# Two graph layers on one core: where the row factors, the group ends and the copies out of the banks are done

## The chip, the cores and the metric

The kernel runs on one core of a Trainium2 chip. The metric is the device time of one execution in microseconds (us). The core has TensorE (PE, matrix products), VectorE (DVE), ScalarE (ACT) and GpSimd (POOL), each working through its own list of instructions in order, and SyncE (SP), whose list here holds only transfers. Transfers are also issued from ScalarE's and GpSimd's lists. All of them run on the core's 16 DMA engines.

## The reference

A graph of 4096 nodes with 512 features goes through two layers. Each takes relu(layernorm(x)) and adds the outcome to x. Layer 0 is an attention with a full score matrix; layer 1 is an attention with 8 heads of 64, whose score is a sum of a row's and a column's number.

```python
def _L0_gnn_ref(x, adj, weight, bias, node_w, edge_w):
    node_att = jax.nn.softmax(x @ node_w, axis=0)
    h = x @ edge_w
    e = h @ h.T
    e = jnp.where(adj > 0, e, NEG_BIG)
    edge_att = jax.nn.softmax(e, axis=1)
    combined_att = node_att * edge_att
    support = x @ weight
    return adj * combined_att @ support + bias

def _L1_gnn_ref(data, connectivity, W, b, src_proj, trg_proj):
    data1 = (data @ W.T + b).reshape(N, H, D)
    src = jnp.einsum('nhd,xhd->nh', data1, src_proj)
    trg = jnp.einsum('nhd,xhd->nh', data1, trg_proj)
    e = src.T[:, :, None] + trg.T[:, None, :]
    e = jnp.where(e >= 0, e, 0.01 * e)
    e = e + connectivity[None, :, :]
    scores = jax.nn.softmax(e, axis=-1)
    out = jnp.einsum('hnm,hmd->hnd', scores, data1.transpose(1, 0, 2))
    return out.transpose(1, 0, 2).reshape(N, H * D)
```

In this model adj is passed as the connectivity of layer 1. All is in 32-bit floats.

## The kernel before

It has four stages, one after the other in time.

**Layer 0, first pass** (until about 745 us): layer norm, the products he_t and sup, the logits of the nodes, then the scores e, of which one half is computed and written to DRAM (e_d), and the masked maxima of the rows (mx_d). The change does not touch it.

**Layer 0, second pass** (about 745 to 1747 us). 8 blocks b of 512 rows (BL), each with 32 steps m of 128 columns. The order of work is written out by hand in `stages` (L332): in loop step s, `load` works for step s+8, `turn` for s+3, `exps` for s+2, `weigh` for s+1 and `gather` for s. `load` fetches scores (et or eb) and the transposed adjacency (a) through SP. `turn` lets TensorE transpose the scores that exist only mirrored. `exps` makes the mask, subtracts the maximum and adds the mask on VectorE (L279, L282, L283) and exponentiates on ScalarE (L285). `weigh` multiplies with the adjacency on VectorE (L291, tile at) and sums the rows on GpSimd (L301, racc). `gather` lets TensorE add at times sup into four PSUM banks po0 to po3 (L324), which are held once (c_p, bufs=1).

At a block's first step `gather` also loads four tiles xt of x through SP and lets GpSimd add the bias to them (L311). At its last step it sums racc with four small products (L318, rs), and VectorE makes sc from rs (L320, L321) and then, straight out of each bank, ot = po * sc + xt (L328); GpSimd's queue writes ot to x1 in DRAM (L330).

**Layer 1, preparation** (to about 1915 us): layer norm of x1, the projected values va, and the factors by which the exponential of leaky relu splits into a maximum of products. Each row's factor z goes to DRAM (z_d).

**Layer 1, main part** (1915 us to the end). A group is 1024 rows (WL) and four of the eight heads; there are 8 groups of 32 steps m. `stages` (L582): `load` for step s+3, `exps` for s+1, `weigh` for s+1, `factors` for s+2, `gather` for s. In each step:

- SP loads a tile e of the adjacency (L452, three buffers);
- ScalarE makes ex (L465, into two PSUM banks held once, so it must wait until VectorE has used the ex before), then e3 and rl of the step after (L474, L477);
- VectorE makes four products pr3, pr0, pr1, pr2, in this order (L489, L486, L489, L489), from z, rl, e3 and ex;
- GpSimd adds pr3 to acc3 (L498), and an accumulating transfer on its queue adds pr0 to acc0 or acc1 (L504);
- TensorE multiplies the products with va into four banks (L516) and sums pr1 and pr2 in dn (L522).

Row factors z are needed as four tiles [128, 1024] per group, the same row in all partitions (`zload`, L461, on GpSimd's queue, 6 buffers): 3 and 0 are asked for with the group's first load, 1 and 2 with its first `factors`.

After a group's last step ScalarE copies the four banks and dn out (os L531, od L532). The rest of the ending is the generator `finish`, of which one piece runs in each step from the fourth of the next group on (L587 to L590): transposes of od and reciprocals rd on VectorE (L543, L544); six sums of the accumulators (L553 to L556) with their copy oa (L558) on ScalarE; again transposes and reciprocals; then four pairs of row tiles, for each a load y of x1 on ScalarE's queue (L567), four transposes (L572), o = pt * rd (L575), two additions of o to y (L577, L578) on VectorE, and the transfer to out on ScalarE's queue (L579). The transposes share one bank, pt. The last group's ending has no next group beside it (L591).

Of the kernel before, what the change touches and what calls it, by code (L numbers as in the profile page):

```python
# [8 lines left out]
FP = mybir.dt.float32  # L9
AF = mybir.ActivationFunctionType  # L10
ALU = mybir.AluOpType
# [4 lines left out]
P = 128  # L16
# [6 lines left out]
def row_bcast(ap, n, offset=0):  # L23

    return bass.AP(tensor=ap.tensor, offset=ap.offset + offset, ap=[[0, P], [1, n]])
# [3 lines left out]
def kernel(  # L29
# [15 lines left out]
    nc = tc.nc  # L45
    N, F = x.shape
    H, D = 8, 64
    HG = 4
    NT = N // P
    KC = F // P  # L50
    BL = 512
    NB = N // BL
    TB = BL // P
# [3 lines left out]
    ident = const.tile([P, P], FP, name="ident")  # L57
# [4 lines left out]
    x1 = dram.tile([N, F], FP, name="x1")  # L62
    z_d = dram.tile([H * NT, P], FP, name="z_d")
# [27 lines left out]
    na = big.tile([P, NT], FP, name="na")  # L91
# [9 lines left out]
    with tc.tile_pool(name="w0", bufs=1) as wp, tc.tile_pool(name="a0", bufs=2) as ap_, tc.tile_pool(  # L101
        name="a0s", bufs=4
    ) as sp, tc.tile_pool(name="a0p", bufs=2, space=PSUM) as pp, tc.tile_pool(
        name="a0l", bufs=1, space=PSUM
# [115 lines left out]
    with tc.tile_pool(name="c_e", bufs=9) as etp, tc.tile_pool(name="c_b", bufs=4) as ebp, tc.tile_pool(  # L220
# [12 lines left out]
        def rows_of(m):  # L233
            return slice(m * P, (m + 1) * P)
# [69 lines left out]
        def gather(b, m):  # L304
            if m == 0:
                blk[b][2] = [p_o.tile([P, F], FP, name=f"po{j}") for j in range(TB)]
                blk[b][3] = []
                for j in range(TB):
                    xt = iop.tile([P, F], FP, name="xt")
                    nc.sync.dma_start(xt, x[rows_of(b * TB + j), :])  # L310
                    nc.gpsimd.tensor_tensor(xt, xt, bias_b, ALU.add)  # L311
                    blk[b][3].append(xt)
            mb, racc, po, xts = blk[b]
            last = m == NT - 1
            if last:
                rs = p_r.tile([P, TB], FP, name="rs")
                for j in range(TB):
                    nc.tensor.matmul(rs[:, j:j + 1], racc[:, j * P:(j + 1) * P], ones, start=True, stop=True)  # L318
                sc = sp.tile([P, TB], FP, name="sc")
                nc.vector.reciprocal(sc, rs)  # L320
                nc.vector.tensor_tensor(sc, sc, na[:, b * TB:(b + 1) * TB], ALU.mult)  # L321
            w = at.pop((b, m))
            for j in range(TB):
                nc.tensor.matmul(po[j], w[:, j * P:(j + 1) * P], sup[:, m, :], start=(m == 0), stop=last)  # L324
            if last:
                for j in range(TB):
                    ot = iop.tile([P, F], FP, name="ot")
                    nc.vector.scalar_tensor_tensor(ot, po[j], sc[:, j:j + 1], xts[j],  # L328
                                                   op0=ALU.mult, op1=ALU.add)
                    nc.gpsimd.dma_start(x1[rows_of(b * TB + j), :], ot)  # L330

        stages = ((load, 8), (turn, 3), (exps, 2), (weigh, 1), (gather, 0))  # L332
        for s in range(-8, len(steps)):
            for f, ahead in stages:
                if 0 <= s + ahead < len(steps):
                    f(*steps[s + ahead])
    l0.close()


# [91 lines left out]
    WL = 1024  # L431
# [3 lines left out]
    with tc.tile_pool(name="e", bufs=3) as ep, tc.tile_pool(name="e3", bufs=2) as e3p, tc.tile_pool(  # L435
# [13 lines left out]
        def load(i, m):  # L449
            b, g = groups[i]  # L450
            e = ep.tile([P, WL], FP, name="e")
            nc.sync.dma_start(e, adj_t[m * P:(m + 1) * P, b * WL:(b + 1) * WL])  # L452
            ra[i, m] = e
            if m == 0:
                zload(i, 3)
                zload(i, 0)

        def zload(i, k):
            b, g = groups[i]
            zs_[i, k] = zp.tile([P, WL], FP, name="z")  # L460
            nc.gpsimd.dma_start(zs_[i, k], row_bcast(z_d, WL, (g * HG + k) * N + b * WL))  # L461

        def exps(i, m):
            x_ = p_x.tile([P, WL], FP, name="ex")
# [41 lines left out]
        def gather(i, m):  # L506
            b, g = groups[i]
            if m == 0:
                pv[i] = ([[p_v.tile([P, BL], FP, name=f"pv{c}{q}") for q in range(HV)] for c in range(2)],
                         p_v.tile([P, BL], FP, name="dn"))  # L510
            v, dn = pv[i]
            flags = dict(start=(m == 0), stop=(m == NT - 1))
            for c, pair in enumerate(((3, 0), (1, 2))):
                for q in range(HV):
                    for r, k in enumerate(pair):
                        nc.tensor.matmul(v[c][q][r * D:(r + 1) * D, :], va[:, m, g * HG + k, :],  # L516
                                         pr[i, m, k][:, q * BL:(q + 1) * BL], **flags)
            for k in (1, 2):
                d = d_m[:, g * HG + k, m:m + 1]
                for q in range(HV):  # L520
                    r = (k - 1) * 2 + q
                    nc.tensor.matmul(dn[r * Q:(r + 1) * Q, :], d.to_broadcast([P, Q]),  # L522
                                     pr[i, m, k][:, q * BL:(q + 1) * BL], **flags)
            for k in range(HG):
                pr.pop((i, m - 1, k), None)
            if m == NT - 1:
                os_ = [[osp.tile([P, BL], FP, name=f"os{c}{q}") for q in range(HV)] for c in range(2)]
                od = osp.tile([P, BL], FP, name="od")
                for c in range(2):
                    for q in range(HV):  # L530
                        nc.scalar.copy(os_[c][q], v[c][q])  # L531
                nc.scalar.copy(od, dn)  # L532
                late[i] = os_, od

        def finish(i):
            b, g = groups[i]
            os_, od = late.pop(i)
            rd = sp.tile([P, WT, HG], FP, name="rd")

            def dens(src, two):  # L540
                pt = p_t.tile([P, WT // HV, P], FP, name="pt")
                for j in range(WT // HV):
                    nc.tensor.transpose(pt[:, j, :], src[:, j * P:(j + 1) * P], ident)  # L543
                nc.vector.reciprocal(rd[:, :, two].rearrange("p (q j) k -> p j k q", q=HV),  # L544
                                     pt.rearrange("p j (k q d) -> p j k q d", k=2, q=HV)[:, :, :, :, 0])

            dens(od, slice(2, 4))
            yield

            ps = p_t.tile([P, BL], FP, name="pt")  # L550
            for q in range(HV):
                s = slice(q * BL, (q + 1) * BL)
                nc.tensor.matmul(ps[q * Q:(q + 1) * Q, :], ones, acc[i, 3][:, s], start=True, stop=True)  # L553
                r = HV + q
                nc.tensor.matmul(ps[r * Q:(r + 1) * Q, :], ones, acc[i, 0][:, s], start=True, stop=False)
                nc.tensor.matmul(ps[r * Q:(r + 1) * Q, :], ones, acc[i, 1][:, s], start=False, stop=True)  # L556
            oa = osp.tile([P, BL], FP, name="oa")
            nc.scalar.copy(oa, ps)  # L558
            yield
            dens(oa, slice(0, 2))  # L560
            yield
            for j in range(0, WT, 2):
                rows = slice(b * WL + j * P, b * WL + (j + 2) * P)
                y = iop.tile([P, 2, HG, D], FP, name="y")

                cols = slice(g * HG * D, (g + 1) * HG * D)
                nc.scalar.dma_start(y, x1[rows, cols].rearrange("(j p) (h d) -> p j h d", p=P, h=HG))  # L567
                pt = p_t.tile([P, 2, HG, D], FP, name="pt")
                for q in range(2):
                    for c in range(2):  # L570
                        s = (j + q) * P % BL
                        nc.tensor.transpose(pt[:, q, 2 * c:2 * c + 2, :].rearrange("p k d -> p (k d)"),  # L572
                                            os_[c][(j + q) * P // BL][:, s:s + P], ident)
                o = sp.tile([P, 2, HG, D], FP, name="o")
                nc.vector.tensor_tensor(o, pt, rd[:, j:j + 2, :].unsqueeze(3).to_broadcast([P, 2, HG, D]),  # L575
                                        ALU.mult)
                nc.vector.tensor_tensor(y[:, :, 0:3, :], y[:, :, 0:3, :], o[:, :, 1:4, :], ALU.add)  # L577
                nc.vector.tensor_tensor(y[:, :, 3, :], y[:, :, 3, :], o[:, :, 0, :], ALU.add)  # L578
                nc.scalar.dma_start(out[rows, cols].rearrange("(j p) (h d) -> p j h d", p=P, h=HG), y)  # L579
                yield  # L580

        stages = ((load, 3), (exps, 1), (weigh, 1), (factors, 2), (gather, 0))  # L582
        for s in range(-3, len(steps)):
            for f, ahead in stages:
                if 0 <= s + ahead < len(steps):
                    f(*steps[s + ahead])
            if s > NT and s % NT == 3:  # L587
                ending = finish(s // NT - 1)
            if s > NT and s % NT >= 3:
                next(ending, None)  # L590
        for _ in finish(len(groups) - 1):  # L591
            pass
# [34 lines left out]
```

## Time and profile before

| | |
|---|---|
| time, median of 3 runs | 3289.96 us (3289.59 to 3289.97) |
| the profiled execution's own time | 3290.54 us |
| its span, first to last instruction | 3288.7 us, granted TensorE clock 0.981 |
| TensorE busy | 3117.9 us (95%) |
| VectorE busy | 2573.5 us (78%) |
| GpSimd busy | 1415.7 us (43%) |
| ScalarE busy | 1195.6 us (36%) |
| product into the banks, L516 | 1025.2 us, 4096 of 610 ns |
| product of the second pass, L324 | 915.2 us, 2048 of 598 ns |
| VectorE products L489 and L486 | 1285 us, 1024 of about 1274 ns |

The span is the time from the first to the last instruction of one profiled execution. A busy share is an average over four stages with different limits, and the busy time of TensorE counts matmuls that are pipelined, so that 95% does not say that TensorE is the limit everywhere. The table of slices shows this: in the second pass DMA is busy for about 0.4 to 0.5 of the time and VectorE for 0.6 to 0.8; in layer 1 both are at 0.8 to 0.9 or more.

```profile
PE   8999999998999999999998869999999999999997
PEld 4554444444444444444444423232323232323332
DVE  3324777776667678788896599898989898999997
ACT  2211111111111111111113256565656666666664
POOL 0001111113434445445454546565656565655554
PEclk9999999998999999999999989999999999999999
DMA  2104666656444444454433179898988898989896
```

Each digit is one fortieth of the span (82 us), in tenths.

### The profile page before, as it was taken

What the parts mean: (1) busy time and instruction counts of PE and PEld (TensorE: products, weight loads), DVE (VectorE), ACT (ScalarE), POOL (GpSimd) and SP (SyncE); (2) the same over time, 40 slices, a digit from 0 to 9 for tenths busy, and PEclk for the clock granted to TensorE, in tenths of its full rate; (3) what the DMA queues carried; (4) which work ended last, traced back from release to release, by engine and by line L of the source; (5) the groups of instructions that cost most, each with busy time, mean ns of one, the idle gap of its engine ahead of it and who ended that gap; (6) DMA issues with size and microseconds to landing.
All of it is one profiled execution on the core that took longest, in us unless ns stands there. A gap on an engine that the chain in (4) does not pass through costs nothing.

```text
span 3288.7 us, 34545 instructions
## 1 busy us (share of the span) xinstructions
PE 3117.9 (95%) x11514; PEld 1291.8 (39%) x11514; DVE 2573.5 (78%) x3593; ACT 1195.6 (36%) x1417; POOL 1415.7 (43%) x1081
## 2 busy tenths in 40 slices
PE   8999999998999999999998869999999999999997
PEld 4554444444444444444444423232323232323332
DVE  3324777776667678788896599898989898999997
ACT  2211111111111111111113256565656666666664
POOL 0001111113434445445454546565656565655554
PEclk9999999998999999999999989999999999999999
DMA  2104666656444444454433179898988898989896
GB/s 74 39 20 158 225 219 229 223 182 211 142 141 155 142 157 159 141 163 157 147 107 103 36 188 223 228 218 225 219 224 217 222 223 224 222 227 219 227 221 161
DMA packets 239250, 577.07 MB, mean 175 GB/s; under 512 B 26048, under 2 KB 51936, under 8 KB 239072
## 3 DMA queue, kind: packets, MB, share of 16 engines
q1 hardware_dynamic: 163680, 357.76, 32.7%
q0 software_dynamic: 55680, 196.13, 26.9%
q10 hardware_dynamic: 19712, 20.98, 2.1%
q8 instruction: 90, 1.47, 0.2%
q14 instruction: 88, 0.72, 0.1%
HBM read 389.02 MB, written 51.53 MB: 134 GB/s over the span
## 4 chain that ended last, share of the span: by engine, by line
PE 62%; DVE 18%; issue 6%; ACT 6%; DMA 4%; POOL 2%; ACTq 0%; DVEq 0%; SPq 0%; POOLq 0%
PE po L324 26%; PE pe L180 14%; DVE pr L489 13%; PE pv L516 8%; ACT e L474 5%; PE ps L136 3%; PE pe L129 3%; PE dn L522 2%; DMA z<-z_d 2%; PE pd L382 2%; PE pt L271 2%; DMA y<-x 1%; POOL pr L387 1%; PE lg L139 1%; DVE d L283 1%
## 5 line engine op out<-in xcount | busy, mean ns | idle before, releaser
L516 PE MATMUL pv<-pr,va 128*64 128x512 f32 x4096 | 1025.2, 610 | 61.5 <-DVE pr L489 40.2
L324 PE MATMUL po<-sup,at 128*128 128x512 f32 x2048 | 915.2, 598 | 45.1 <-DVE at L291 45.1
L498 POOL TENSOR_TENSOR acc<-acc,pr 128x1024 f32<-128x1024 f32 x240 | 570.3, 2376 | 434.2 <-DVE pr L489 434.0
L489 DVE SCALAR_TENSOR_TENSOR pr<-z,g_m,ex 128x1024 f32<-128x1024 f32 x512 | 631.4, 1273 | 41.9 <-DMA z<-z_d 41.9
L516 PEld LDWEIGHTS pv<-pr,va 128*64 128x64 f32 x4096 | 359.4, 137 | 686.0 <-issue 378.7
L324 PEld LDWEIGHTS po<-sup,at 128*128 128x128 f32 x2048 | 380.2, 192 | 479.7 <-issue 403.7
L301 POOL TENSOR_TENSOR racc<-racc,ex 128x512 f32<-128x512 f32 x240 | 354.7, 1478 | 467.4 <-ACT ex L285 466.8
L285 ACT ACTIVATE ex<-d 128x512 f32<-128x512 f32 x256 | 161.3, 630 | 829.0 <-DVE d L283 829.0
L180 PE MATMUL pe<-he_t 128*128 128x512 f32 (+3 forms) x1152 | 455.8, 557 | 0.1
L465 ACT ACTIVATE ex<-e 128x1024 f32<-128x1024 f32 x256 | 263.1, 1028 | 456.6 <-DVE pr L489 356.9
L486 DVE SCALAR_TENSOR_TENSOR pr<-rl,gd_m,ex 128x1024 f32<-128x1024 f32 x256 | 326.0, 1274 | 29.1 <-ACT ex L465 29.1
L489 DVE SCALAR_TENSOR_TENSOR pr<-z,g_m,e 128x1024 f32<-128x1024 f32 x256 | 327.6, 1280 | 0.0
L477 ACT ACTIVATE rl<-z,ngd_m,d_m 128x1024 f32<-128x1024 f32 x256 | 314.1, 1227 | 26.9 <-DMA z<-z_d 26.9
L180 PEld LDWEIGHTS pe<-he_t 128*128 128x128 f32 x1152 | 212.9, 190 | 234.5 <-issue 222.5
L474 ACT ACTIVATE e<-e,ld_m 128x1024 f32<-128x1024 f32 x256 | 290.0, 1133 | 5.0 <-DMA z_d<-zs 5.0
L283 DVE TENSOR_TENSOR d<-d,mk 128x512 f32<-128x512 f32 x256 | 273.7, 1069 | 8.8
L522 PE MATMUL dn<-pr,d_m 128*32 128x512 f32 x2048 | 273.8, 607 | 0.0
L184 POOL DMA_DIRECT2D e_d<-es x144 | 79.2, 550 | 351.3 <-ACT es L183 345.8
L282 DVE TENSOR_TENSOR d<-pt,mb 128x512 f32<-128x512 f32 (+2 forms) x136 | 87.4, 643 | 172.6 <-PE pt L271 172.6
L183 ACT COPY es<-pe 128x512 f32<-128x512 f32 (+2 forms) x144 | 79.3, 551 | 376.2 <-PE pe L180 376.2
L504 POOL DMA_DIRECT2D acc<-pr x240 | 208.2, 868 | 5.0 <-DVE pr L486 4.0
L291 DVE TENSOR_TENSOR at<-ex,a 128x512 f32<-128x512 f32 x256 | 190.5, 744 | 0.5
(116 smaller groups left out, 2182.9 us busy)
## 6 DMA issues: line engine op xcount, KB each, us to landing
e<-in_adj_t_dram SPq DMA_DIRECT2D x256, 512.0 KB, 4.5
acc<-pr POOLq DMA_DIRECT2D x256, 512.0 KB, 4.9
a<-in_adj_t_dram SPq DMA_DIRECT2D x256, 256.0 KB, 3.4
ar<-in_adj_dram SPq DMA_DIRECT2D x120, 256.0 KB, 3.1
e_d<-es POOLq DMA_DIRECT2D x120, 256.0 KB, 2.8
ac<-in_adj_t_dram SPq DMA_DIRECT2D x112, 256.0 KB, 3.2
eb<-e_d SPq DMA_DIRECT2D x28, 1024.0 KB, 5.8
et<-e_d SPq DMA_DIRECT2D x112, 256.0 KB, 3.5
```

The source lines that it names most:

```text
L180: nc.tensor.matmul(pe[:, :w], he_t[:, k, rows], he_t[:, k, cols], start=(k == 0), stop=(k == KC - 1))
L283: nc.vector.tensor_tensor(d, d, mk, ALU.add)
L301: nc.gpsimd.tensor_tensor(racc, racc, e, ALU.add)
L324: nc.tensor.matmul(po[j], w[:, j * P:(j + 1) * P], sup[:, m, :], start=(m == 0), stop=last)
L465: nc.scalar.activation(x_, ra.pop((i, m)), AF.Exp)
L474: nc.scalar.activation(x_, ra[i, m], AF.Exp, bias=ld_m[:, h + 3, m:m + 1])
L477: nc.scalar.activation(r, zs_[i, 0], AF.Relu, bias=ngd_m[:, h, m:m + 1], scale=d_m[:, h, m:m + 1])
L486: nc.vector.scalar_tensor_tensor(w, rl.pop((i, m)), gd_m[:, h, m:m + 1], x_, op0=ALU.add, op1=ALU.mult)
L489: nc.vector.scalar_tensor_tensor(w, zs_[i, k], g_m[:, h + k, m:m + 1], e3.pop((i, m)) if k == 3 else x_, op0=ALU.max, op1=ALU.mult)
L498: nc.gpsimd.tensor_tensor(acc[i, 3], acc[i, 3], w, ALU.add)
L516: nc.tensor.matmul(v[c][q][r * D:(r + 1) * D, :], va[:, m, g * HG + k, :], pr[i, m, k][:, q * BL:(q + 1) * BL], **flags)
L522: nc.tensor.matmul(dn[r * Q:(r + 1) * Q, :], d.to_broadcast([P, Q]), pr[i, m, k][:, q * BL:(q + 1) * BL], **flags)
```

## The change

Second pass of layer 0:

- The four loads of xt and their additions on GpSimd move from a block's first step to its ninth (m = 8).
- At the block's last step ScalarE copies each bank po to a tile oc. VectorE's part (sc, and oc = oc * sc + xt) and the transfer to x1 are deferred: a list `left` is worked off by a new `finish`, one row tile per loop step behind `weigh`, from the third step of the next block on; what is left after the last block follows the loop.

Layer 1, main part:

- z is loaded through SP, where the adjacency's loads are, and no longer through GpSimd's queue; 0 is asked for before 3.
- dn is copied to od not with the four banks but by `finish`, which now starts one step after the group's last, at the end of that step, and goes on from the fourth. The copy oa is moved one step behind its sums.
- The values are scaled by ScalarE: for each row tile two transposes, and in the step after four activations of [128, 64] that take rd as their scale (`AF.Copy`). VectorE's multiplication and two additions go.
- The residual is added by an accumulating transfer on GpSimd's queue, from x1 into o, after each second tile. The transfer from o to out stands on SP, one step after that.

```diff
@@ layer 0, second pass @@
+            if m == TB * 2:
                 for j in range(TB):
                     xt = iop.tile([P, F], FP, name="xt")
                     nc.sync.dma_start(xt, x[rows_of(b * TB + j), :])
...
-                sc = sp.tile([P, TB], FP, name="sc")
-                nc.vector.reciprocal(sc, rs)
-                nc.vector.tensor_tensor(sc, sc, na[:, b * TB:(b + 1) * TB], ALU.mult)
...
-                    ot = iop.tile([P, F], FP, name="ot")
-                    nc.vector.scalar_tensor_tensor(ot, po[j], sc[:, j:j + 1], xts[j],
-                                                   op0=ALU.mult, op1=ALU.add)
-                    nc.gpsimd.dma_start(x1[rows_of(b * TB + j), :], ot)
+                    oc = iop.tile([P, F], FP, name="oc")
+                    nc.scalar.copy(oc, po[j])
+                    left.append((b * TB + j, oc, rs if j == 0 else None, xts[j]))
+
+        def finish():
+            t, oc, rs, xt = left.pop(0)
+            b, j = divmod(t, TB)
+            if j == 0:
+                sc = sp.tile([P, TB], FP, name="sc")
+                nc.vector.reciprocal(sc, rs)
+                nc.vector.tensor_tensor(sc, sc, na[:, b * TB:(b + 1) * TB], ALU.mult)
+                scale[b] = sc
+            nc.vector.scalar_tensor_tensor(oc, oc, scale[b][:, j:j + 1], xt, op0=ALU.mult, op1=ALU.add)
+            nc.gpsimd.dma_start(x1[rows_of(t), :], oc)
...
+                if f is weigh and left and s % NT > 1:
+                    finish()
+        while left:
+            finish()
@@ layer 1, main part @@
             if m == 0:
+                zload(i, 0)
                 zload(i, 3)
-                zload(i, 0)
...
-            nc.gpsimd.dma_start(zs_[i, k], row_bcast(z_d, WL, (g * HG + k) * N + b * WL))
+            nc.sync.dma_start(zs_[i, k], row_bcast(z_d, WL, (g * HG + k) * N + b * WL))
...
-                nc.scalar.copy(od, dn)
-                late[i] = os_, od
+                late[i] = os_, dn
 
         def finish(i):
...
+            od = osp.tile([P, BL], FP, name="od")
+            nc.scalar.copy(od, dn)
+            yield
...
+            yield
             oa = osp.tile([P, BL], FP, name="oa")
             nc.scalar.copy(oa, ps)
-            yield
             dens(oa, slice(0, 2))
             yield
-            for j in range(0, WT, 2):
...
-                nc.scalar.dma_start(y, x1[rows, cols].rearrange("(j p) (h d) -> p j h d", p=P, h=HG))
...
-                nc.vector.tensor_tensor(o, pt, rd[:, j:j + 2, :].unsqueeze(3).to_broadcast([P, 2, HG, D]),
-                                        ALU.mult)
-                nc.vector.tensor_tensor(y[:, :, 0:3, :], y[:, :, 0:3, :], o[:, :, 1:4, :], ALU.add)
-                nc.vector.tensor_tensor(y[:, :, 3, :], y[:, :, 3, :], o[:, :, 0, :], ALU.add)
-                nc.scalar.dma_start(out[rows, cols].rearrange("(j p) (h d) -> p j h d", p=P, h=HG), y)
+            for t in range(WT + 3):
+                if 0 < t <= WT:
+                    if t % 2:
+                        o = iop.tile([P, 2, HG, D], FP, name="o")
+                    for r, k in enumerate(ORDER):
+                        nc.scalar.activation(o[:, (t - 1) % 2, k, :], pt[:, r, :], AF.Copy,
+                                             scale=rd[:, t - 1, r:r + 1])
+                    if t % 2 == 0:
+                        nc.gpsimd.dma_start(o, part(x1, b * WT + t - 2, cols), accum_op=ALU.add)
+                if t > 2 and t % 2:
+                    nc.sync.dma_start(part(out, b * WT + t - 3, cols), oo)
+                if t % 2 == 0:
+                    oo = o
+                if t < WT:
+                    q, j = divmod(t, WT // HV)
+                    pt = p_t.tile([P, HG, D], FP, name="pt")
+                    for c in range(2):
+                        nc.tensor.transpose(pt[:, 2 * c:2 * c + 2, :].rearrange("p k d -> p (k d)"),
+                                            os_[c][q][:, j * P:(j + 1) * P], ident)
                 yield
...
-            if s > NT and s % NT == 3:
+            if s >= NT and s % NT == 0:
                 ending = finish(s // NT - 1)
-            if s > NT and s % NT >= 3:
+            if s >= NT and s % NT not in (1, 2):
                 next(ending, None)
```

More of the change, by code (lines that the diff above doesn't have):

```diff
@@ L326, in gather @@
                 for j in range(TB):
-                    ot = iop.tile([P, F], FP, name="ot")
-                    nc.vector.scalar_tensor_tensor(ot, po[j], sc[:, j:j + 1], xts[j],
-                                                   op0=ALU.mult, op1=ALU.add)
-                    nc.gpsimd.dma_start(x1[rows_of(b * TB + j), :], ot)
+                    oc = iop.tile([P, F], FP, name="oc")
+                    nc.scalar.copy(oc, po[j])
+                    left.append((b * TB + j, oc, rs if j == 0 else None, xts[j]))
+        left, scale = [], {}
+        def finish():
[8 more added lines that the diff above has]
+            nc.gpsimd.dma_start(x1[rows_of(t), :], oc)
         stages = ((load, 8), (turn, 3), (exps, 2), (weigh, 1), (gather, 0))
@@ L527, in gather @@
                 os_ = [[osp.tile([P, BL], FP, name=f"os{c}{q}") for q in range(HV)] for c in range(2)]
-                od = osp.tile([P, BL], FP, name="od")
                 for c in range(2):
@@ L531, in gather @@
                         nc.scalar.copy(os_[c][q], v[c][q])
-                nc.scalar.copy(od, dn)
-                late[i] = os_, od
+                late[i] = os_, dn
         def finish(i):
             b, g = groups[i]
-            os_, od = late.pop(i)
+            os_, dn = late.pop(i)
+            od = osp.tile([P, BL], FP, name="od")
+            nc.scalar.copy(od, dn)
+            yield
             rd = sp.tile([P, WT, HG], FP, name="rd")
@@ L556, in finish @@
                 nc.tensor.matmul(ps[r * Q:(r + 1) * Q, :], ones, acc[i, 1][:, s], start=False, stop=True)
+            yield
             oa = osp.tile([P, BL], FP, name="oa")
             nc.scalar.copy(oa, ps)
-            yield
             dens(oa, slice(0, 2))
             yield
-            for j in range(0, WT, 2):
-                rows = slice(b * WL + j * P, b * WL + (j + 2) * P)
-                y = iop.tile([P, 2, HG, D], FP, name="y")
-                cols = slice(g * HG * D, (g + 1) * HG * D)
-                nc.scalar.dma_start(y, x1[rows, cols].rearrange("(j p) (h d) -> p j h d", p=P, h=HG))
-                pt = p_t.tile([P, 2, HG, D], FP, name="pt")
-                for q in range(2):
-                    for c in range(2):
[L571 to L574, printed above, removed]
-                nc.vector.tensor_tensor(o, pt, rd[:, j:j + 2, :].unsqueeze(3).to_broadcast([P, 2, HG, D]),
-                                        ALU.mult)
-                nc.vector.tensor_tensor(y[:, :, 0:3, :], y[:, :, 0:3, :], o[:, :, 1:4, :], ALU.add)
-                nc.vector.tensor_tensor(y[:, :, 3, :], y[:, :, 3, :], o[:, :, 0, :], ALU.add)
-                nc.scalar.dma_start(out[rows, cols].rearrange("(j p) (h d) -> p j h d", p=P, h=HG), y)
@@ new lines, in finish @@
+            cols = slice(g * HG * D, (g + 1) * HG * D)
+            o = None
+            for t in range(WT + 3):
[14 more added lines that the diff above has]
+                    pt = p_t.tile([P, HG, D], FP, name="pt")
+                    for c in range(2):
+                        nc.tensor.transpose(pt[:, 2 * c:2 * c + 2, :].rearrange("p k d -> p (k d)"),
+                                            os_[c][q][:, j * P:(j + 1) * P], ident)
@@ L580, in finish, with part @@
                 yield
+        def part(ap, t, cols):
+            return ap[t * P:(t + 2) * P, cols].rearrange("(j p) (h d) -> p j h d", p=P, h=HG)
         stages = ((load, 3), (exps, 1), (weigh, 1), (factors, 2), (gather, 0))
```

## The prediction

> **What bounds the kernel now.** I read the busy rows, then the waits of layer 1 (1905 us to the end), then timelines around its group ends, then stretches of the second pass of layer 0, and last the end of the program.
>
> Waits in layer 1 (who waited for whom: us in total, times, longest):
>
> ```profile
> ACT ex L465 <- DVE y L578: 99.8, 28, 5.0
> ...
> DVE pr L489 <- DMA z<-z_d: 41.9, 8, 6.8
> ...
> DVE pr L486 <- ACT ex L465: 29.1, 42, 1.8
> ...
> DVE y L577 <- DMA y<-x: 10.8, 5, 3.1
> ...
> DVE rd L544 <- PE pt L543: 9.1, 5, 4.4
> ```
>
> Timeline at the end of the first group (start, us, what, idle before it):
>
> ```profile
> 2229.39 1.39 POOL L461 DMA_DIRECT2D z<-z_d  x2
> ...
> 2238.93 1.40 POOL L461 DMA_DIRECT2D z<-z_d  x2
> 2239.35 1.28 DVE L489 SCALAR_TENSOR_TENSOR pr<-z,g_m,e 128x1024 f32<-128x1024 f32 x1
> 2239.95 1.24 ACT L477 ACTIVATE rl<-z,ngd_m,d_m 128x1024 f32<-128x1024 f32 x1 [3.15 <-DMA z<-z_d]
> ...
> 2249.03 2.55 DVE L489 SCALAR_TENSOR_TENSOR pr<-z,g_m,ex 128x1024 f32<-128x1024 f32 x2 [5.61 <-DMA z<-z_d]
> ```
>
> In mid-group VectorE issues four products back to back: L489 starts at 2229.81, 2234.58, 2239.35, a step of 4.77 us. TensorE needs 4.58 us for its step when nothing holds it (L516 starts 2086.49, 2091.07, 2095.64). So VectorE sets the pace, and DMA is close behind. Stretches (PE, PEld, DVE, ACT, POOL busy; clock; DMA share; GB/s):
>
> ```profile
> 2174.00:2198.00 24.00, 24.00 (x123) 8.27 (x120) 24.00 (x21) 16.29 (x16) 16.12 (x11) 1.00 0.93 221
> ...
> 2242.00:2247.00 5.00, 2.58 (x12) 0.48 (x8) 1.28 (x1) 4.71 (x8) 0.53 (x1) 0.90 1.05 311
> 2247.00:2252.00 5.00, 1.95 (x5) 0.58 (x5) 2.97 (x3) 0.39 (x1) 0.00 (x0) 0.50 0.62 249
> ```
>
> The step costs 0.93 of the DMA engines; at the group end they are full, VectorE and TensorE stand, and the clock falls to 0.50.
>
> From the first L489 of layer 1 (1915.13) to that of the last step (3256.31) pass 1341.2 us; 255 steps of 4.77 are 1216.4. The 124.8 over are seven group ends of **17.8 us**: z about 6.0 (41.9/7), pr waiting for ex about 4.2 (29.1/7), the end's own VectorE work 6.6 (four times 0.69+0.56+0.28 from L575, L577, L578, and two reciprocals of 0.26), the rest y and rd (most of their totals lies in the last group).
>
> Second pass of layer 0, same columns:
>
> ```profile
> 1014.00:1030.00 16.00, 11.45 (x27) 4.65 (x26) 15.79 (x16) 1.89 (x3) 12.80 (x11) 1.00 0.83 290
> 1030.00:1139.00 109.00, 109.00 (x326) 52.87 (x325) 75.59 (x123) 18.27 (x29) 38.73 (x31) 1.00 0.39 126
> 1139.00:1156.00 17.00, 12.45 (x29) 5.13 (x28) 16.75 (x17) 1.89 (x3) 13.79 (x11) 1.00 0.85 302
> ```
>
> TensorE is the bound, full except for **4.55 us** at each block end. Its cause, on the timeline:
>
> ```profile
> 882.13 0.18 DVE L320 RECIPROCAL sc<-rs 128x4 f32<-128x4 f32 x1 [3.46 <-PE rs L318]
> ...
> 883.17 3.33 DVE L328 SCALAR_TENSOR_TENSOR ot<-po,sc,xt 128x512 f32<-128x512 f32 x4 [0.66 <-PE po L324]
> ```
>
> VectorE stands before the reciprocal, drains four banks, and only then makes the next block's weights, slowed by POOL's four bias adds (L283 takes 1.64 there, else 0.69).
>
> **What the Trainium skill says.** "GPSIMD Engine Reference", section Key points: GpSimd shares its SBUF interfaces with VectorE and contends with instructions of two SBUF inputs; the 1.64 against 0.69 agrees. "DMA: Bandwidth & Descriptors", section SWDGE vs HWDGE vs iDMA: transfers issued from GpSimd and from SP feed different internal queues of the same DMA engines, taken in turn, so moving z gives it a turn beside the accumulations and not new bandwidth; the 1.05 share at the group end agrees that there is none to spare. "TensorE: Matmul & The Clock Gate", part 1: an idle array runs at half clock until busy again; 0.50 agrees.
>
> **The change, part by part.**
>
> *z through SP.* Now z3 and z0 issue at 2229.4, z1 and z2 at 2238.9, behind POOL's add (2.37) and accumulation. After it z0 and z3 follow the load of the next group's first tile, freed by ex at 2226.2; z1 follows rl of the last step (ends 2233.2), z2 its first product (ends 2235.9). The loads are queued past these two waits, but ex of that step ends at 2235.7 anyway: no cost. A 512 KB load costs about 1.53 us of all engines (queue 1 moves 357.76 MB in 32.7% of the span: 1.58) and an accumulation the rest of 0.93 x 4.77, 2.9. Taken in turn, SP has half: 3.1 us a transfer. e0, z0, z3, e1, z1, z2 from 2226.2 end at 2241.4 (z1) and 2244.4 (z2), plus 1.4 us of latency (e lands after 4.5). VectorE wants z1 at 2241.7 and z2 1.2 later: it waits 1 and then 1.8. I take **3.0** per end in place of 6.0; bounds 1 (stalled products leave SP the whole bandwidth) and 6.
>
> *Values by ScalarE, residual by transfer.* VectorE loses 6.1 us per end and keeps 0.5. ScalarE gets four activations of 64 elements in each of eight steps. No row shows such a one. L72 (one element, bias by pointer) takes 0.289, two back to back 0.48, so 0.24 apart; 128-element copies take 0.266. "ScalarE: Activation LUTs", Rules for kernel authors, prices 0.3 us plus 0.83 ns an element, an estimate of 0.35. Four cost 0.8 to 1.4; I take 1.0. ScalarE's step ends 3.4 us after VectorE's last product (2215.49, rl until 2218.84), and its next ex may start 4.9 after it: 1.5 free. Hidden, **0**; at worst 0.3 in each of eight steps, 2.4. ScalarE no longer stands for y (99.8 us) nor for oa right after its matmuls, so most of the 4.2 goes.
>
> *What is late next: TensorE at the reciprocals.* od is now copied behind ex, e3 and rl of the next step, so the first dn matmul starts about 4.0 us after the step's last product and ends at 5.1, where 4.6 was seen (2081.9 to 2086.5). Transposes of od (0.66) and the six sums (1.7) still come in the stream; TensorE gains only 0.19 a step. The first reciprocal then holds VectorE 0.6, the second 2.0: **2.6** (bounds 1 and 5). Two transposes in each later step add 0.3, less 0.19 gained: below what the product buffers allow.
>
> *out on SP.* The accumulation of o is issued 4.6 us into its step and runs behind acc; from the 4.9 of acc I let it land 10 us into it. out, on SP one step later, waits for it, and behind it stands the next load, due to be issued 4.1 earlier. It then lands at about 15.4 (10.1 + 0.8 for out + 4.5), just when e3 wants it: 0 by this sum. But DMA work here exceeds the step: ten steps of 4.41 and four pairs of 2.2 (0.75 to write, 1.44 to accumulate 256 KB, half of acc) make 53 us in 47.7, and the accumulation queues behind it. I take **2.5** per end, bounds 0 and 6.
>
> New end: 3.0 + 0.5 + 2.6 + 2.5 = 8.6; gain 9.2, times seven, **-64**.
>
> *Second pass.* ScalarE copies each bank in 0.58 while TensorE still fills the next, so the following block can start at once, and VectorE no longer stands for rs: all 4.55 go, -32 over seven. VectorE is about 5 us ahead (weights made 946.8 to 947.5, used from 952.6); ex standing behind the copies costs it some 2.6 of that. The four deferred products (0.75 each) lie in steps where VectorE needs 3.2 of TensorE's 3.5. The bias adds move to step 8 and slow VectorE by some 3.6 us: in blocks 2 to 7, where the lead is spent, 2 us of TensorE each, +12. Net **-20**, bounds -31 and -8.
>
> *Program's end.* The last group has no cover. Before, from the first value transposes (3269.6) to the end were 19.1 us, paced by y:
>
> ```profile
> 3284.70 0.56 DVE L577 TENSOR_TENSOR y<-y,o 128x384 f32<-128x384 f32 x1 [3.08 <-DMA y<-x]
> ```
>
> After: 1.75 us per tile (transposes 0.45, four activations 1.0 to 1.2, handovers). Pair 0 is ready at 3273.1, added by 3278.0 (4.9), written by 3280.7 (2.7 as out takes now); only then is its buffer free for pair 2. Pair 3 follows at 3284.2, is ready at 3287.7, added 3292.6, written 3295.3: **+7**, bounds +3 and +12.
>
> *First z of layer 1.* It comes sooner, but VectorE is busy scaling va until 1915.2 (L420): 0.
>
> **Sum:** -64 - 20 + 7 = -77. The profiled execution took 3290.54 (span 3288.7 and 1.8 around it), 0.6 above the median of 3289.96. So **3213** against the median.
>
> **Rivals.**
> - *z stays late.* DMA is full at the ends whichever queue issues. Waits of z and the ex behind it stay (7.5, not 3.0): 4.5 x 7 = +32, **3245**. For it: 1.05; against: z issues 3 to 6 us sooner. 0.17.
> - *Clean ends.* Waits overlap, and only 4 us per end remain: -32, **3181**; with the whole 32 of the second pass about 3169. 0.16.
> - *Slower: SP blocked by out.* If the accumulation of o lands 15 us into its step, each of the 28 outs starves e3 by 5 us: 140 where I took 17.5, **3335**. It decides from 3.4 us per out ((77+17.5)/28). For it: DMA over 100% there; against: only e3 waits, with two steps of lead, and each stall lets DMA catch up. 0.05.
> - *Waits merely change their names:* unchanged, **3290**. 0.02.
>
> The forecast has 0.60, its own range 3190 to 3237. Range for 8 in 10: 3168 (clean ends) to 3256 (late z, upper costs). A measurement tells 0.2% (7 us) from no change. Faster 0.93, same 0.02, slower 0.05.
>
> **What would show it.** Right: L489 waits for z about 3 us an end; no ex waiting for VectorE's y; rd waits near 2.6; groups of about 161 us; no TensorE gap at block ends and small ones near step 8. Wrong: e3 waiting for e in the odd steps after a group's start (out blocks SP), activations over 0.37 us apart, or z waits of 6.

## The result and the profile after

The changed kernel takes **3241.43 us** (median of 4 runs, 3236.11 to 3249.65), the kernel before 3289.78 beside it (3284.51 to 3289.97): a ratio of 0.9859, 95% interval 0.9836 to 0.9882. The forecast was 3213: the time went down by 48 where I had 77. It lies above the forecast's own range (3190 to 3237), inside the wider one (3168 to 3256) and nearest to the rival "z stays late" (3245), whose wait, however, is not what the trace shows. The profiled execution of the changed kernel took 3236.11, the lowest of its four, with a span of 3234.2. So the trace shows 5 us less than the median, and where I compare traces I use spans.

I split the span by two instructions: the first pr3 of layer 1 (the L489 of before is L504 now) and that of the last step.

| | before | after | change | forecast |
|---|---|---|---|---|
| start to the first pr3 | 1915.1 | 1884.6 | -30.6 | -20 |
| first to last pr3 (255 steps, 7 group ends) | 1341.2 | 1309.4 | -31.8 | -64 |
| last pr3 to the end of the span | 32.4 | 40.2 | +7.8 | +7 |

The second pass gave more than forecast, the program's end cost what was forecast, and the group ends gave half. Over the 1216.4 us of 255 bare steps, 93.0 are left, **13.3 us per group end**, where 17.8 were and 8.6 were forecast.

The waits of layer 1 in the profile after, from 1900 us on (who waited for whom: us in total, times, longest):

```profile
ACT e L489 <- DMA e<-in_adj_t_dram: 93.7, 41, 6.8
...
DVE rd L562 <- PE pt L561: 28.3, 16, 4.4
...
DVE pr L501 <- ACT ex L480: 25.0, 26, 1.5
...
DVE pr L504 <- ACT e L489: 23.7, 8, 4.4
...
DVE pr L504 <- DMA z<-z_d: 10.8, 9, 1.5
```

ScalarE's 99.8 for y are gone and the wait for z fell from 41.9 to 10.8. But VectorE still waits 25.0 for ex and now 23.7 for e3, which it had not waited for. Behind both stands the first line: ScalarE, which makes ex, e3 and rl in order, waits 93.7 us for tiles of the adjacency. SP, which asks for them, waited for this (same view, SP's queue):

```profile
SPq L467 <- ACT ex L480: 830.5, 191, 7.6
SPq L592 <- DMA o<-x: 318.2, 32, 33.6
```

The first line is the healthy one: SP stands until a buffer of e is free, as before. The second is new: 32 transfers to out (L592) stand until the residual has been added into o. The timeline in the second group's start (start, us, what, idle before it) shows the consequence:

```profile
2113.98 1.20 POOL L590 DMA_DIRECT2D o<-x  x1 [0.84 <-ACT o L587]
...
2117.83 1.15 ACT L489 ACTIVATE e<-e,ld_m 128x1024 f32<-128x1024 f32 x1 [2.39 <-DMA e<-in_adj_t_dram]
...
2122.96 0.39 SPq L592 DMA_DIRECT2D out_dram<-o  x1
...
2125.16 1.19 POOL L590 DMA_DIRECT2D o<-x  x1 [0.86 <-ACT o L587]
...
2131.61 1.15 ACT L489 ACTIVATE e<-e,ld_m 128x1024 f32<-128x1024 f32 x1 [5.01 <-DMA e<-in_adj_t_dram]
...
2132.86 1.29 DVE L504 SCALAR_TENSOR_TENSOR pr<-z,g_m,e 128x1024 f32<-128x1024 f32 x1 [2.55 <-ACT e L489]
...
2134.85 0.40 SPq L592 DMA_DIRECT2D out_dram<-o  x1
```

The addition asked for at 2113.98 lets SP go on at 2122.96, 9.0 us later; the next takes from 2125.16 to 2134.85, 9.7. The two before them took 6.0 and 8.6. Behind each out are the next loads of the adjacency, and e3 at 2131.61 has waited 5.01 for one of them. The instruction's own row says the same for all (min/median/max):

```profile
L590 POOL DMA_DIRECT2D o<-x x32: 1181/1201/1424, 2093.6 to 3225.2; - x32
...
DMA to landing us min/median/max: 4.1/8.5/9.9
```

In the second pass TensorE runs through the block ends. The stretches that answer to the two of before (11.45 busy in 16, 12.45 in 17; columns as there):

```profile
992.00:1008.00 16.00, 16.00 (x46) 7.63 (x45) 12.51 (x19) 4.80 (x9) 2.91 (x2) 1.00 0.40 141
1118.00:1134.00 16.00, 16.00 (x45) 7.61 (x44) 12.73 (x19) 4.93 (x9) 4.43 (x3) 1.00 0.51 172
```

What it loses instead lies at the moved bias additions, in the timeline of the block that begins in the second of these stretches:

```profile
1155.41 6.46 POOL L312 TENSOR_TENSOR xt<-xt,bias_b 128x512 f32<-128x512 f32 x4
1155.92 1.75 DVE L291 TENSOR_TENSOR at<-ex,a 128x512 f32<-128x512 f32 x1
...
1164.15 3.70 PE L322 MATMUL po<-sup,at 128*128 128x512 f32 x8 [2.19 <-DVE at L291]
```

While GpSimd adds, VectorE's 0.69 becomes 1.75, and TensorE stands once for 2.19.

### The profile page after: what moved, and what is told of

Same layout as the page of the kernel before. It is cut to its first block, busy times and chain, and to the rows that moved or that the text cites. A ratio compares the mean times of both kernels' runs of the same rounds, so it can differ in the third digit from the quotient of the medians.

```text
span 3234.2 us, 34905 instructions
## 1 busy us (share of the span) xinstructions
PE 3074.8 (95%) x11514; PEld 1260.4 (39%) x11514; DVE 2539.0 (79%) x3497; ACT 1265.0 (39%) x1705; POOL 1423.4 (44%) x1081
## 4 chain that ended last, share of the span: by engine, by line
PE 55%; DVE 17%; DMA 10%; ACT 9%; issue 8%; POOL 1%; SPq 0%; DVEq 0%; POOLq 0%; ACTq 0%
PE po L322 21%; PE pe L180 14%; DVE pr L504 11%; DMA e<-in_adj_t_dram 7%; ACT e L489 6%; PE pv L531 5%; PE ps L136 4%; PE pe L129 3%; PE pd L397 2%; PE dn L537 2%; PE pt L271 2%; DVE at L291 2%; DVE d L282 1%; DMA o<-x 1%; POOL pr L402 1%
## 5 line engine op out<-in xcount | busy, mean ns | idle before, releaser
L531 PE MATMUL pv<-pr,va 128*64 128x512 f32 x4096 | 982.8, 602 | 33.3 <-DVE pr L504 21.9
L322 PE MATMUL po<-sup,at 128*128 128x512 f32 x2048 | 908.8, 595 | 23.5 <-DVE at L291 23.5
L504 DVE SCALAR_TENSOR_TENSOR pr<-z,g_m,ex 128x1024 f32<-128x1024 f32 x512 | 631.8, 1274 | 14.2 <-DMA z<-z_d 10.8
L531 PEld LDWEIGHTS pv<-pr,va 128*64 128x64 f32 x4096 | 330.3, 137 | 628.7 <-issue 385.2
L322 PEld LDWEIGHTS po<-sup,at 128*128 128x128 f32 x2048 | 379.4, 191 | 452.4 <-issue 410.9
L301 POOL TENSOR_TENSOR racc<-racc,ex 128x512 f32<-128x512 f32 x240 | 342.6, 1427 | 429.1 <-ACT ex L285 427.4
L504 DVE SCALAR_TENSOR_TENSOR pr<-z,g_m,e 128x1024 f32<-128x1024 f32 x256 | 327.6, 1280 | 24.2 <-ACT e L489 23.7
L489 ACT ACTIVATE e<-e,ld_m 128x1024 f32<-128x1024 f32 x256 | 291.0, 1137 | 102.2 <-DMA e<-in_adj_t_dram 96.9
```

The source lines that it names most:

```text
L301: nc.gpsimd.tensor_tensor(racc, racc, e, ALU.add)
L489: nc.scalar.activation(x_, ra[i, m], AF.Exp, bias=ld_m[:, h + 3, m:m + 1])
L504: nc.vector.scalar_tensor_tensor(w, zs_[i, k], g_m[:, h + k, m:m + 1], e3.pop((i, m)) if k == 3 else x_, op0=ALU.max, op1=ALU.mult)
```

## The experiments

Two theories for the group ends. **A: order on SP.** Each out stands in front of the loads; what hurts is SP waiting for the addition. **B: volume.** The DMA engines have more to do than the step is long, so tiles come late wherever out stands. And as a question of its own: what each part of the change is worth alone.

The excess per group end is taken for each as above: (last pr3 minus first pr3 minus 1216.4) / 7, from the profiled execution.

| kernel | median, us | ratio to before, 95% | excess per end |
|---|---|---|---|
| before | 3289.78 | 1 | 17.8 |
| changed | 3241.43 | 0.9859 (0.9836 to 0.9882) | 13.3 |
| third buffer of o only | 3235.33 | 0.9844 (0.9828 to 0.9861) | 13.2 |
| out one step later | 3209.54 | 0.9754 (0.9740 to 0.9769) | 10.2 |
| out two steps later | 3186.76 | 0.9691 (0.9675 to 0.9707) | 6.6 |
| od copied with the banks | 3217.78 | 0.9780 (0.9765 to 0.9794) | 11.0 |
| out two steps later and od with the banks | 3161.05 | 0.9612 (0.9597 to 0.9626) | 3.0 |
| before, with z on SP | 3244.61 | 0.9863 (0.9848 to 0.9877) | 10.6 |
| before, with the second pass and z on SP | 3212.66 | 0.9768 (0.9752 to 0.9784) | 10.8 |
| before, with the second pass | 3259.50 | 0.9906 (0.9891 to 0.9921) | 17.4 |

### Out two steps later

```diff
-    tc.tile_pool(name="io1", bufs=2) as iop
+    tc.tile_pool(name="io1", bufs=3) as iop
...
-            for t in range(WT + 3):
+            for t in range(WT + 5):
...
-                if t > 2 and t % 2:
-                    nc.sync.dma_start(part(out, b * WT + t - 3, cols), oo)
+                        oo.append(o)
+                if t > 4 and t % 2:
+                    nc.sync.dma_start(part(out, b * WT + t - 5, cols), oo.pop(0))
```

> The changed kernel, with the transfer to out asked for two steps later on SP (three buffers for o instead of two), so that the accumulation has landed when SP reaches it. Same bytes, same accumulations. If the late loads of e come from SP standing before out (theory A), ScalarE's waits for e fall from 94 us in layer 1 to below 15, the group ends lose about 7 us each, and the time is near 3192. If the DMA engines are simply full near a group end (theory B), e stays late: waits of 60 us or more, and the time stays within 12 us of 3241.

3186.76 us (3183.84 to 3194.41). Waits of layer 1 in its profile, first of the engines, then of SP:

```profile
DVE rd L562 <- PE pt L561: 33.4, 16, 4.4
...
DVE pr L504 <- DMA z<-z_d: 12.0, 12, 1.6
...
ACT e L489 <- DMA e<-in_adj_t_dram: 7.7, 9, 1.6
```

```profile
SPq L467 <- ACT ex L480: 1015.2, 244, 7.3
SPq L593 <- DMA o<-x: 116.0, 32, 33.5
```

ScalarE's wait for tiles fell from 93.7 to 7.7 (the views of the runs begin at 1880; from there the changed kernel has 96.9) and the two waits of VectorE behind it left the list. The same stretch at the second group's start, 2090 to 2138, first of the changed kernel, then of this one (columns as in the stretches above):

```profile
2090.00:2138.00 48.00, 45.75 (x236) 12.68 (x232) 42.10 (x36) 33.90 (x55) 33.66 (x22) 1.00 1.01 224
```

```profile
2090.00:2138.00 48.00, 48.00 (x258) 13.57 (x254) 48.00 (x41) 37.95 (x58) 36.22 (x25) 1.00 1.04 248
```

The DMA engines are as full (1.04 against 1.01), and VectorE works all 48.00 us in place of 42.10. The loads of e land no sooner than in the changed kernel (median 7.1 us against 6.5 in this stretch); they are only asked for in time. So volume makes the transfers land late in both kernels, but it alone does not starve ScalarE: B falls, A holds.

### Out one step later

The same, with `if t > 3 and t % 2 == 0` and `t - 4` over `range(WT + 3)`.

> The changed kernel, with the transfer to out one step later on SP (half of the delay of the run with two steps; three buffers for o). The accumulations landed 6 to 10 us after their issue; one step gives 4.8 us. If SP's standing is the cause (theory A), it now stands about 5 us instead of 10 per out, the loads are hardly late: ScalarE's waits for e below 40 us, 3195 to 3210. If it is a matter of where the bytes fall (theory B), no order: above 3225.

3209.54 us (3202.76 to 3211.26): between the two others, with an excess of 10.2 between 13.3 and 6.6. ScalarE waits 42.5 us for tiles (20 times), a little over the 40 that A gave, and SP 237.4 for the additions. The loss follows the time that SP stands, as A says.

### The third buffer only

Both kernels with a later out also have a third buffer for o, which the later out needs. This one has the buffer and nothing else:

```diff
-    tc.tile_pool(name="io1", bufs=2) as iop
+    tc.tile_pool(name="io1", bufs=3) as iop
```

> The changed kernel with three buffers for o in place of two, and out where the change put it. A (only the place of out counts): as the changed kernel, 3236 to 3250, and ScalarE waits some 90 us for tiles of the adjacency. C (the third buffer, which both kernels with a later out also have, brought part of their gain): below 3225. In the last group the third buffer may take up to 5 us off the program's end (one wait of ScalarE of 5.0 for a buffer of o is seen there) under both.

3235.33 us (3231.86 to 3237.49), just below the range that A gave. Main part: 13.2 per end against 13.3, and ScalarE waits 95.9 for tiles. From the last pr3 to the end it takes 35.7 us where the changed kernel takes 40.2: a gain of 4.5 in the last group alone. So the buffer brought the later outs nothing in the main part.

### od copied with the banks

The changed kernel copies dn to od one step later, behind ex, e3 and rl. Put back:

```diff
-                late[i] = os_, dn
+                od = osp.tile([P, BL], FP, name="od")
+                nc.scalar.copy(od, dn)
+                late[i] = os_, od
```

> The changed kernel, with dn copied to od directly behind the four banks as in the kernel before. The first reciprocal then waits less (2.5 us to about 1) and dn no longer waits for od: 2 to 3 us per end, 3222 to 3227, if TensorE's lag at the reciprocals costs what it shows. If the late e hides it (the same time is then waited for e), within 5 us of 3241.

3217.78 us (3213.77 to 3221.35), somewhat less than expected. Waits of layer 1:

```profile
ACT e L489 <- DMA e<-in_adj_t_dram: 94.2, 37, 6.7
...
DVE rd L562 <- PE pt L561: 12.8, 9, 4.4
```

The reciprocals' wait fell from 28.3 to 12.8, of which 7.9 lie in the last group's end, and the wait for tiles stayed at 94.2. By the medians the edit is worth 24 us, by the two spans 15 (3234.2 to 3219.4), close to the 15.5 that the wait lost; the profiled execution was the fastest of the changed kernel and the slowest of this one. Above the later out, where the runs scatter less, it is worth 26 by the medians and 25 by the spans (below).

### Parts of the change alone

The kernel before with the changed second pass:

```diff
+            if m == TB * 2:
                 for j in range(TB):
                     xt = iop.tile([P, F], FP, name="xt")
...
-                    nc.vector.scalar_tensor_tensor(ot, po[j], sc[:, j:j + 1], xts[j],
-                                                   op0=ALU.mult, op1=ALU.add)
+                    nc.scalar.copy(oc, po[j])
+                    left.append((b * TB + j, oc, rs if j == 0 else None, xts[j]))
```

> The kernel before, with the change's second pass of layer 0 alone. By the two traces it gave 26 us in the pass and 3 to 4 more up to the first product of layer 1. If the parts are independent: 3260, that is 30 us below before. If part of this is only taken back by layer 1 (its first loads), 3270.

3259.50 us (3257.86 to 3260.38): -30. Its first pr3 starts at 1885.66, 29.5 earlier than in the kernel before.

The kernel before with z through SP:

```diff
             if m == 0:
+                zload(i, 0)
                 zload(i, 3)
-                zload(i, 0)
...
-            nc.gpsimd.dma_start(zs_[i, k], row_bcast(z_d, WL, (g * HG + k) * N + b * WL))
+            nc.sync.dma_start(zs_[i, k], row_bcast(z_d, WL, (g * HG + k) * N + b * WL))
```

> The kernel before, with z loaded through SP and 0 before 3, nothing else. My sum took 3.0 us of waiting per group end in place of 6.0 and the waits of ex behind it with them, 4.5 in all: 3258. If a z that is early only hands the wait to the loads of e behind it on SP, the time is above 3275. If nothing takes its place: 7.5 per end, 3237.

3244.61 us (3244.02 to 3246.71): -45, nearly the whole gain of the change, and more than I had expected from a sum over its waits. Its waits of layer 1:

```profile
DVE pr L486 <- ACT ex L465: 14.1, 35, 0.7
...
ACT e L474 <- DMA e<-in_adj_t_dram: 9.2, 8, 2.3
...
DVE pr L489 <- DMA z<-z_d: 7.9, 9, 1.4
```

z fell from 41.9 to 7.9, ex from 29.1 to 14.1. Four transfers moved to another queue, with 0 asked for before 3, took 7.2 of the 17.8 us from each end; the move and the new order were not tried apart.

Both together, with the old group end:

> The kernel before with the second pass of the change and z on SP; the group end as before (values and residual on VectorE, y and out on ScalarE's queue). If the parts add up (30 and 45): 3215. Then the new group end as written costs about 26 us against the old one, where I had taken it for a gain. If the parts overlap and the new group end is no loss, 3240.

3212.66 us (3210.09 to 3215.43): the parts add, 77 us against 30 + 45. So the rest of the change, the new group end, cost 29 us as it was written (3241.43 against 3212.66), although it takes 6 us of VectorE's work from each end. By the two spans it is 24, of which 7.4 lie in the program's end (40.2 against 32.8 from the last pr3).

### Both repairs

Out two steps later and od with the banks, in one kernel:

> The changed kernel with both edits: out two steps later, od copied behind the banks. Of the 25 us that VectorE waits at the reciprocals inside the program some 5 remain: 3187 - 20 = 3167. If the lag of TensorE comes back at the second reciprocal (six sums): 3178.

**3161.05 us** (3160.93 to 3162.40), a ratio of 0.9612 (0.9597 to 0.9626): faster than both kernels, and than I expected. Main part of the changed kernel and of this one, as stretches:

```profile
1885.00:3194.00 1309.00, 1255.70 (x6357) 388.88 (x6358) 1225.15 (x1035) 888.00 (x1030) 824.05 (x530) 1.00 0.92 227
```

```profile
1885.00:3123.00 1238.00, 1228.86 (x6358) 364.30 (x6360) 1222.07 (x1037) 888.64 (x1031) 825.04 (x530) 1.00 0.95 240
```

VectorE's work is the same, 1225 and 1222 us; it fills 94% of one and 98.7% of the other. What went is waiting. Against the second pass and z with the old end (3212.66) the new end is now worth 52 us.

The program's end is still the longer one (36.7 us from the last pr3, 32.4 before). In this run the last group's value transposes also get the four banks that are free by then:

```diff
+                    if tail:
+                        pt = p_v.tile([P, BL], FP, name=f"pv{j % 2}{j // 2}")
+                        pt = pt[:, 0:HG * D].rearrange("p (h d) -> p h d", h=HG)
```

> As the run with both edits, and in the last group's ending, which nothing covers, the value transposes go to the four banks that are free then, instead of one. Eight turns of 1.75 us become eight of about 1.0 on ScalarE: 4 to 6 us less than that run, 3162. If the accumulations' landing and the buffers of o set the pace there, less than 2.

3161.70 us (3159.94 to 3162.96): no difference between the medians. In the profiled executions the end took 34.0 in place of 36.7, less than the 4 to 6 expected, and the main part, which the edit does not touch, took 3.0 more. The timeline shows what took the place of the transposes:

```profile
3137.89 5.03 ACT L587 ACTIVATE o<-pv,rd 128x64 f32<-128x64 f32 x24 [1.09 <-DVE rd L562]
...
3148.74 1.75 ACT L587 ACTIVATE o<-pv,rd 128x64 f32<-128x64 f32 x8 [5.82 <-DMA out_dram<-o]
```

24 activations run through, and the last eight wait 5.82 us for a buffer of o. So most of what the banks save is waited for again: the sequence add, write, free sets the pace there, as the expectation had it for its other case.

## Why the prediction was right or wrong

**Right: the direction, and that z and the second pass pay.** VectorE set the pace, z's queue was a large cost, and moving it took 7.2 of the 17.8 us from each end. **Wrong in sign: the new group end.** z alone was worth 45 us where its expectation, from the same sum, had 32, and the second pass 30 where I had 20. That left some 25 of the forecast 77 for the new group end with the program's end; it cost 29. That the total missed by only 28 is thus in part luck: two parts gave 23 us more than I had, and the third missed by 54.

**Wrong: one term, "out on SP", 2.5 us per end.** I wrote "from the 4.9 of acc I let it land 10 us into it", that is 5.4 us after its issue, and from there e3 got its tile just in time. The addition takes 8.5 (median), 3.1 more. The 4.9 was a median over the whole program. In the seven stretches from the first to the last addition of a group end acc, too, lands after 7.1 to 7.6 (medians), and a load of e after 6.3 to 7.8 where I took 4.5. The kernel before has 5.0 and 4.2 at the second group's start (2105 to 2150 us), so its trace did not show this load: the change makes it.

ScalarE's wait for tiles is (93.7 - 7.7) / 28 = 3.1 us per out. That this equals the 3.1 of the addition is partly chance, as the loads land later as well. At VectorE it came to 3.4 (e3) and 3.6 (ex) per end, **7.0 in place of 2.5**; removing it took 13.3 to 6.6, which is 6.7. I had worked out that there are 53 us of DMA work in 47.7 and given the surplus one allowance, while the landings within the end that is shown grow from out to out (6.0, 8.6, 9.0, 9.7), as a surplus that adds up would make them. The sign that I had named for this, e3 waiting for e in every second step, is there (2117.83 and 2131.61). My slower rival had this mechanism with 5 us per out; measured is 7.0 / 4 = 1.75, half of the 3.4 from which it would have decided. The upper bound of 6 was too low.

**z: too much, 3.0 for 1.5.** The waits are 10.8 / 7 = 1.5. (I used 1.53 us of all engines for a load, while the figures beside it give 1.58; that moves z1 by half a microsecond.) I had seen two waits of 1 and 1.8 coming and the trace has 1.11 and 1.20 at the first end. The Trainium skill, "DMA: Bandwidth & Descriptors", section SWDGE vs HWDGE vs iDMA, as I used it, gives z a turn beside the accumulations: these two waits agree, though z is also asked for earlier and no run separates the two. The rival "z stays late" falls. That ScalarE no longer stands for y was to take most of the 4.2 of ex; alone, z on SP took it to 14.1 / 7 = 2.0 with the old y still there. Half of that wait was thus a follow-up of the late z.

**rd: right.** (28.3 - 7.9) / 7 = 2.9 where 2.6 were taken. What I did not draw from it: most of the cost comes from where the change puts the copy od, and can be taken back: with the old place (12.8 - 7.9) / 7 = 0.7 is left.

**The activations: right, hidden.** Four take 0.90 to 0.93 together; I had 1.0. **The clean end**, 0.5 of own work: right. The terms z 1.5, own 0.5, rd 2.9 and out 7.0, with 0 for the activations, leave 1.4 of the 13.3 unnamed: 0.5 is VectorE waiting for a product buffer that TensorE holds (3.2 / 7), the rest I have not traced.

**The second pass: -30.6 for -20.** The stalls went as worked out. TensorE's waits for at in the pass, first before, then after (the longest is the first block's start):

```profile
PE po L324 <- DVE at L291: 45.1, 15, 13.4
```

```profile
PE po L322 <- DVE at L291: 23.5, 7, 11.9
```

Without the longest 31.7 and 11.6: a gain of 20.1, and 11.6 left where I had 12. The other 10 are in no term of mine: the products themselves take 6.4 less (L324 915.2, L322 908.8), preparation 2.7 less, the start 1.5 less. Most of the 6.4 is the clock: an idle TensorE falls to half clock until it is busy again (the Trainium skill, "TensorE: Matmul & The Clock Gate", part 1), and the traces agree. After the first block's start the granted clock is 0.50 for some 3.4 us at four block ends of before (near 898, 1396, 1519 and 1638 us), and once after the change, behind a bias addition (near 1522). Three of these fewer are about 5 us by an estimate from these figures (3 x 3.4 / 2). This error hid a third of what the group ends missed.

**The program's end: +7.8 for +7**, by the path that was given: the third buffer takes 4.5 of it away.

In sum 7 x (13.3 - 8.6) = +33, -10.6 and +0.8 make 23 of the 28 us by which the median lies above the forecast; the last 5 are the distance of the profiled execution from its median.

## What to carry to other kernels

Here a transfer that waited for another transfer held every later one of its queue (SP stood 318 us, and 116 with out two steps later). Such a transfer belongs on a queue behind which nothing urgent stands, or so late that its wait is over when it is reached. Price it with the landing time under the load that the change itself will make at that place (8.5 here), not with a similar row's median over the whole program (4.9). Where the engines for transfers have more work than the step is long, let the surplus add up from one to the next before a slack is called enough. And look at every edit of a bundle alone: here two of them carried the gain, and the third, which removed the most work, cost 29 us until its order was mended, when it gave 52.

## What was not expected of the hardware

- An accumulating transfer of 256 KB into o landed after 8.5 us (median, 4.1 to 9.9), one of 512 KB into acc after 5.2 in the same kernel. Most of the difference goes with the place: in the stretches in which o is added, acc takes 7.1 to 7.6. What makes o the slower one even there, with half the bytes, was not tried: the pattern of x1 in DRAM, or its place behind another accumulation in the same queue. Issuing it took GpSimd 1.20 us, issuing that of acc 0.85.
- Activations of [128, 64] take 0.305 each, but four in a row 0.93, some 0.21 apart ((0.93 - 0.305) / 3). The 24 in a row of the last run, 5.03 in all, give the same.
- The runs of the changed kernel lie 13.5 us apart (3236.11 to 3249.65), those with out two steps later 10.6, those with both repairs 1.5. Where tiles arrive just too late, small differences in the transfers decide; that this is the cause is a guess, and the run with the third buffer only, where ScalarE waits as long for tiles (95.9), speaks against it: its runs lie 5.6 apart.
